# Turned rows and exponentials by way of HBM for nearly all sequences, in an attention and mixture-of-experts kernel

## The chip, the core and the metric

The kernel runs on one core of a Trainium2 chip. The metric is the device time of one execution in microseconds; each kernel is executed several times and the median counts. All times below are in microseconds unless marked ns.

## The reference

One layer with a norm ahead of each half: causal attention with one head, then a mixture of experts with a shared expert. There are 8 sequences of 512 tokens, 256 features each, all in float32.

```
x = x + attention(layernorm(x), Wq, Wk, Wv)      # softmax(q k' / 16, causal) v
h = layernorm(x)
shared = (silu(h Wg') * (h Wu')) Wd'              # inner size 512
probs  = sigmoid(h Wr' + bias)                    # 8 experts, the best two are taken
routed = sum over the two: weight * ((silu(h G_e) * (h U_e)) D_e)
x = x + shared + routed
```

## The kernel before

**Stages.** After an opening in which Wq and Wk are folded into one matrix, a Python loop (L630) goes through the 8 sequences `b`. For each it does the attention row block by row block (`attend`, L458; 4 blocks of 128 tokens), normalizes the result into `hn`, turns it into `hT` (features on the partitions), prepares the next sequence (its scores, its values `v`), finds the two experts of each token (`route`, L486) and the places of its rows in a table by expert (`places_of`, L540), and sends each row twice to HBM by indirect DMAs of GpSimd (`dispatch`, L557), into `rows_h`. When all sequences are done, `plan_tiles` (L189) works out which expert takes which 256 or 128 rows, and the routed experts run over them (L900, L923); `fetch` (L841) brings their rows and `fetch_w` (L831) their weights. Last come the shared expert of the sequences 4 to 6 and the sums.

**Units.** The shared expert of half a sequence is one unit (`shared_beside`, L564): 32 matmuls L578, the tanh form of silu on ScalarE (L589) and VectorE (L593, L596), 16 matmuls L605 and two copies L609 (each matmul instruction stands in the trace as two). The sequences 0, 1, 2, 3 and 7 give two units each to the list `waiting`. Each sequence takes one unit from the list and runs it between its own pieces. Sequence 0 has no older one, so it takes the first half of its own. Before the change, sequence 6 takes none; sequence 7 takes one, and three are left for L817, after the last `dispatch` and beside the plan.

**Two ways to turn.** A tile is turned either on TensorE (`turned`, L331, transposes L340 and a copy on ScalarE L341) or by way of HBM: it is stored (`stored_rows`, L370), loaded in 32-row blocks by four DMAs (`loaded_blocks`, L373) and finished by a transpose of 32x32 squares on VectorE (`turn_squares`, L382). The exponentials of the softmax likewise: on TensorE within `attend` (L463, L465), or with `ex_d`, `loaded_squares` (L418) and `turn_exponentials` (L430, L434). Three sets say which sequences go by HBM:

- `VIA` = 1 to 5 and 7: their `hn` goes by HBM, at least its first half.
- `WHOLE` = 1 to 5: both halves of `hn` do.
- `SENT` = 1 to 6: their exponentials do. Then all four scores of a sequence are done one stage earlier, behind the attention of the sequence before (L716), and `attend` finds its exponentials turned.

So before the change sequences 0 and 6 turn all of `hn` on TensorE, sequence 7 turns the second half there, and sequences 0 and 7 turn their exponentials there, with their scores between (L669).

**Order.** A scheduler orders the instructions of each engine when the kernel is built; `tc.issue_after(x)` sets what an instruction must stand behind. Each engine issues in that order. SP issues nearly all plain DMAs of the loop, GpSimd the indirect ones and the power of the norm (L179), ScalarE the expert weights. PSUM tiles come from three small pools: `ps_o` with 2 buffers holds the attention's output `av` (L472), freed by L476 on VectorE, and also the routing's tiles, the places `pp` (L544, L545) and the units' `po`; `ps_m` has 4 and `ps_t` 2. `marks["turned"]` holds back L476 behind the routing's last step on VectorE (`run`, L535).

**Start of the experts.** `fetch(0)` reads rows from `rows_h`, and so waits for all indirect stores and the rows of blanks (L199). The first turn L873 stands behind the last unit's L596 on VectorE; the next expert weights (L838) stand behind the last unit's L609 on ScalarE, and behind these the load of the table for silu.

## Time and profile before

| | us |
|---|---|
| median of 11 runs | 678.93 (678.24 to 680.88) |
| the profiled execution | 681.02 |
| its span, first to last instruction | 679.2 |
| TensorE matmul busy | 666.2 |
| VectorE busy | 302.4 |
| GpSimd busy | 157.6 |
| ScalarE busy | 150.9 |

The span is divided into 40 equal slices of 17 in the page; each digit is the busy share of a slice in tenths, PEclk the clock that TensorE was granted, DMA the mean share of the 16 DMA engines.

```profile
PE   6999999999999999999999999999999999999997
DVE  4668778787787753222122122121221112223765
PEclk9999999999999999999999999999999999999999
DMA  6643877768663266975653553554534557724875
```

The loop over the sequences fills about 13 slices (to 231), the units left over two more, the routed experts from 263 on the next 20 or so, and the late shared expert and the sums the rest. TensorE is busy throughout; VectorE is so only in the loop and at the end. A profile line gives start, busy time, engine, line and operation, then the tile written and those read, the shape, and how many; in brackets stands the idle time before it and what ended that.

### The profile page before, as it was taken

The numbers are of one execution on the slowest core, as the hardware profiler recorded it, in microseconds if no ns is written. First come the engines' busy times: TensorE is split into PE (matmuls) and PEld (weight loads), VectorE is DVE, ScalarE is ACT, GpSimd is POOL, SyncE is SP. The second block draws the span as 40 slices with busy tenths as digits, with TensorE's granted clock in tenths as the row PEclk, the third lists the DMA queues.
The fourth block names the chain that finished last, engine by engine and source line by source line (L and its number), as shares of the span: only waits on it lengthen the run. The fifth ranks groups of instructions, "written<-read, shape, count | busy, mean of one in ns | idle before, by whom it ended". The sixth has DMA issues, their size and how long they took to land.

```text
span 679.2 us, 10379 instructions
## 1 busy us (share of the span) xinstructions
PE 666.2 (98%) x3178; PEld 543.9 (80%) x3178; DVE 302.4 (45%) x1002; ACT 150.9 (22%) x359; POOL 157.6 (23%) x210
## 2 busy tenths in 40 slices
PE   6999999999999999999999999999999999999997
PEld 5677877777776888888888888888888899994556
DVE  4668778787787753222122122121221112223765
ACT  2432321322213222111211111111112111111110
POOL 3102451523516530021211211211121122121000
PEclk9999999999999999999999999999999999999999
DMA  6643877768663266975653553554534557724875
GB/s 232 180 119 110 237 201 179 207 171 221 203 155 110 91 190 166 305 203 164 187 179 119 164 174 113 177 162 127 179 132 130 158 171 225 249 97 144 239 233 176
DMA packets 152809, 118.48 MB, mean 174 GB/s; under 512 B 109648, under 2 KB 131280, under 8 KB 152752
## 3 DMA queue, kind: packets, MB, share of 16 engines
q1 hardware_dynamic: 133552, 57.00, 32.4%
q10 hardware_dynamic: 12912, 43.53, 18.5%
q0 software_dynamic: 6288, 17.24, 7.0%
q8 instruction: 28, 0.46, 0.3%
q14 instruction: 29, 0.24, 0.1%
HBM read 82.79 MB, written 34.95 MB: 173 GB/s over the span
## 4 chain that ended last, share of the span: by engine, by line
PE 78%; DVE 8%; DMA 5%; SPq 3%; POOL 2%; issue 2%; ACTq 1%; ACT 1%; DVEq 0%; POOLq 0%
PE po L923 17%; PE pg L900 17%; PE pu L900 17%; PE pg L578 6%; PE pg L1011 3%; PE po L605 3%; PE po L1070 3%; PE pu L1011 3%; PE pm L395 2%; PE sc L442 2%; PE av L472 2%; PE pm L407 2%; SPq L377 2%; SPq L424 2%; DMA squares<-exd 1%
## 5 line engine op out<-in xcount | busy, mean ns | idle before, releaser
L886 DVE TENSOR_TENSOR hidp<-pu,sgt 128x512 f32<-128x512 f32 x56 | 38.6, 691 | 210.2 <-PE pu L900 203.7
L929 POOL DMA_INDIRECT rows_y<-y,to x56 | 53.7, 959 | 266.0 <-ACT y L928 141.4
L900 PE MATMUL pg<-hTt,w 128*128 128x256 f32 x448 | 105.9, 379 | 0.8 <-ACT sgt L885 0.8
L900 PE MATMUL pu<-hTt,w 128*128 128x256 f32 x448 | 105.8, 379 | 0.0
L923 PE MATMUL po<-w_down,hidp 128*128 x448 | 101.3, 379 | 0.0
L900 PEld LDWEIGHTS pg<-hTt,w 128*128 128x128 f32 x448 | 85.0, 190 | 12.7 <-ACT sgt L885 1.2
L900 PEld LDWEIGHTS pu<-hTt,w 128*128 128x128 f32 x448 | 85.1, 190 | 11.6
L923 PEld LDWEIGHTS po<-w_down,hidp 128*128 128x128 f32 x448 | 85.0, 190 | 11.5
L578 PE MATMUL pg<-hT,w_sh 128*128 128x256 f32 x320 | 74.0, 383 | 0.2 <-ACT hT L341 0.2
L559 POOL DMA_INDIRECT rows_h<-hn,at x64 | 63.3, 988 | 22.7 <-issue 17.6
L885 ACT ACTIVATE sgt<-pg 128x512 f32<-128x512 f32 x67 | 40.0, 598 | 126.7 <-PE pg L900 119.8
L578 PEld LDWEIGHTS pg<-hT,w_sh 128*128 128x128 f32 x320 | 59.5, 190 | 9.5 <-ACT sg L589 0.8
L928 ACT COPY y<-po 128x256 f32<-128x256 f32 x67 | 24.8, 372 | 151.5 <-PE po L923 143.2
L179 POOL TENSOR_TENSOR rstd<-var,minus_half 128x1 f32<-128x1 f32 (+1 forms) x43 | 26.9, 634 | 129.4 <-DVE var L178 73.7
L605 PE MATMUL po<-w_sh,hid 128*128 128x256 f32 x160 | 37.3, 383 | 0.2
L442 PE MATMUL sc<-xT,qT 128*128 128x128 f32 (+3 forms) x128 | 37.4, 434 | 0.0
L605 PEld LDWEIGHTS po<-w_sh,hid 128*128 128x128 f32 x160 | 29.4, 190 | 6.1 <-DVE hid L596 2.1
L395 PE MATMUL pm<-xT,w_qk 128*128 128x512 f32 x64 | 29.9, 592 | 0.0
L886 DVE TENSOR_TENSOR khid<-pu,sgt 128x512 f32<-128x512 f32 x11 | 7.6, 691 | 48.9 <-PE pu L900 48.9
L407 PE MATMUL pm<-wv_sb,xT 128*128 128x256 f32 x128 | 29.0, 380 | 0.2 <-ACT xT L341 0.2
L407 PEld LDWEIGHTS pm<-wv_sb,xT 128*128 128x128 f32 x128 | 24.2, 190 | 6.1 <-issue 2.6
L172 DVE BATCH_NORM_STATS2 bnst<-total 128x6 f32<-128x256 f32 x64 | 25.2, 411 | 8.5 <-DMA total<-in_x_dram 8.5
(156 smaller groups left out, 760.7 us busy)
## 6 DMA issues: line engine op xcount, KB each, us to landing
w<-in_gate_w_dram ACTq DMA_DIRECT2D x41, 512.0 KB
w<-in_up_w_dram ACTq DMA_DIRECT2D x41, 512.0 KB
yl<-rows_y SPq DMA_DIRECT2D x32, 256.0 KB
h<-rows_h SPq DMA_DIRECT2D x112, 64.0 KB
w_down<-in_down_w_dram SPq DMA_DIRECT2D x8, 512.0 KB
out_dram<-total SPq DMA_DIRECT2D x32, 128.0 KB
total<-in_x_dram SPq DMA_DIRECT2D x7, 512.0 KB
xnd<-xn SPq DMA_DIRECT2D x6, 512.0 KB
```

The source lines that it names most:

```text
L395: nc.tensor.matmul(pm, lhsT=w_qk[:, k, ts(m, P)], rhs=xT[:, k, :], start=(k == 0), stop=(k == ND - 1),)
L407: nc.tensor.matmul(pm, lhsT=xT[:, k, ts(c, P)], rhs=wv_sb[:, k, :], start=(k == 0), stop=(k == ND - 1),)
L442: nc.tensor.matmul(sc[:, :n], lhsT=qT[:, k, ts(i, P)], rhs=xT[:, k, :n], start=(k == 0), stop=(k == ND - 1),)
L559: lands(nc.gpsimd.indirect_dma_start(out=rows_h[:, :], out_offset=bass.IndirectOffsetOnAxis(ap=at[:, r, c : c + 1], axis=0), in_=hn[:, c, ...
L578: mm = nc.tensor.matmul(pg[:, w, :], lhsT=w_sh[:, ds(w * gu + k * I + m * P, P)], rhs=hT[:, k, at], start=(k == 0), stop=(k == ND - 1),)
L605: nc.tensor.matmul(po, lhsT=hid[:, m, ts(j, P)], rhs=w_sh[:, ds(2 * gu + m * D, D)], start=(m == 0), stop=(m == NI - 1),)
L885: nc.scalar.activation(sg, pg, AF.Silu)
L886: return nc.vector.tensor_tensor(out=hid, in0=pu, in1=sg, op=ALU.mult).ins
L900: nc.tensor.matmul(dst[:, m, :], lhsT=w[:, i, k, ts(m0 + m, P)], rhs=hT[:, ts(k, n * P)], start=(k == 0), stop=(k == ND - 1),)
L923: nc.tensor.matmul(po, lhsT=hid[:, m, ts(j, P)], rhs=w_down[:, ds(w + m * D, D)], start=(m == 0), stop=(m == NI - 1),)
L929: nc.gpsimd.indirect_dma_start(out=rows_y[:, :], out_offset=bass.IndirectOffsetOnAxis(ap=to[:, j : j + 1], axis=0), in_=y, in_offset=None,)
L1011: nc.tensor.matmul(dst, lhsT=w_sh[:, ds(off + k * I + m * P, P)], rhs=hT[:, k, :], start=(k == 0), stop=(k == ND - 1),)
```

## The change

The sets change: `hn` goes by HBM whole for the sequences 0 to 6, and not at all for 7; exponentials go by HBM for 1 to 7. Sequence 6 now also takes a unit from the list, so two are left at the end in place of three. With that the special cases for sequence 6 go (its routing was run through at once, L776), and sequence 7, which now finds its scores done and has no sequence behind it, gets some of its own: no projection in its attention (`ahead_T is not None`), places of sequence 6 at row block 2, and the unit beside sequence 7 held back behind its first four matmuls (one half of `pg`, step `(0, 1)`) and no longer behind its eighth. All eight indirect stores of sequence 6 now stand at the last row block of sequence 7 (L700), in place of two at block 2 and six at block 3.

```
-    VIA = [b for b in range(1, B) if b != B - 2]
-    WHOLE = range(1, B - 2)
-    SENT = range(1, B - 1)
+    VIA = range(B - 1)
+    WHOLE = range(B - 1)
+    SENT = range(1, B)
...
             if i:
-                with tc.issue_after(summed.ins) if i != NT // 2 or xb is not total[B - 1] else nullcontext():
+                with tc.issue_after(summed.ins):
                     normalize(hn[:, i - 1, :D], xb, i - 1, mv, rstd)
...
-                with tc.issue_after(marks["turned"]) if r and b < B - 2 else nullcontext():
+                with tc.issue_after(marks["turned"]) if r and b < B - 1 else nullcontext():
                     nc.vector.tensor_reduce(out=top, in_=prob, axis=AX.X, op=ALU.max)
...
-                    elif (m, w) == (NI // 2 - 1, 1) and halfway is not None:
+                    elif (m, w) == (0, 1) and halfway is not None:
                         held = halfway
...
                 if b in SENT:
                     sc = exs[i]
-                    if i % 2 == 0:
+                    if i % 2 == 0 and ahead_T is not None:
...
-                if i == (1 if b in SENT else 2) and placed is not None:
+                if i == (1 if b in SENT and ahead_T is not None else 2) and placed is not None:
                     placed()
...
-                        with tc.issue_after(marks["blocks"]) if b else nullcontext():
+                        with tc.issue_after(marks["blocks"]) if b in WHOLE else nullcontext():
                             stored = nc.sync.dma_start(out=ex_d[b + 1][0], in_=ex[0]).ins
...
                 next(routing)
-                if b < B - 2:
+                if b < B - 1:
                     yield
                 mask = next(routing)
...
                 choice = chosen()
                 next(choice)
-                if b + 2 == B:
-                    for _ in choice:
-                        pass
...
             if b + 1 < B:
 
-                if b + 2 < B:
-                    def behind():
+                def behind():
...
-                    added = shared_beside(
-                        *waiting.pop(0), midway=midway, behind=behind, early=choice,
+                added = shared_beside(
+                    *waiting.pop(0), midway=midway, behind=behind, early=choice,
...
```

The last two pieces move `behind`, `midway` and the call of `shared_beside` out of a condition that left out sequence 6; their bodies stay.

More of the change, by code (lines that the diff above doesn't have):

```diff
@@ L786, with midway @@
             if b + 1 < B:
-                if b + 2 < B:
-                    def behind():
-                        nonlocal exT
-                        with tc.issue_after(marks["hid"]), tc.issue_after(marks["first"]):
-                            exT = turn_exponentials(squares)
-                        next(choice, None)
-                        marks["squares"], marks["turned"] = marks["turned"], marks["run"]
-                    def midway():
-                        if b + 3 < B:
-                            with tc.issue_after(marks["squares"]):
-                                rows, _ = first_norm(*coming)
-                            with tc.issue_after(marks["sent"]):
-                                blocks[b + 3], _ = sent_to_blocks(xn_d[b + 3], rows)
-                    added = shared_beside(
-                        *waiting.pop(0), midway=midway, behind=behind, early=choice,
-                        rows_from=1 if b in WHOLE else NI,
-                        steps=((NI // 2, 1), (NI - 1, 1)) if b in WHOLE else ((0, 1), (1, 1)),
-                    )
+                def behind():
+                    nonlocal exT
+                    with tc.issue_after(marks["hid"]), tc.issue_after(marks["first"]):
+                        exT = turn_exponentials(squares)
+                    next(choice, None)
+                    marks["squares"], marks["turned"] = marks["turned"], marks["run"]
+                def midway():
+                    if b + 3 < B:
+                        with tc.issue_after(marks["squares"]):
+                            rows, _ = first_norm(*coming)
+                        with tc.issue_after(marks["sent"]):
+                            blocks[b + 3], _ = sent_to_blocks(xn_d[b + 3], rows)
+                added = shared_beside(
+                    *waiting.pop(0), midway=midway, behind=behind, early=choice,
+                    rows_from=1 if b in WHOLE else NI,
+                    steps=((NI // 2, 1), (NI - 1, 1)) if b in WHOLE else ((0, 1), (1, 1)),
+                )
                 xT = ahead_T
```

## The prediction, made before the changed kernel was run

> **What bounds the kernel now.** I read the page first, then TensorE's waits, then the order of time on TensorE (PE), VectorE (DVE), ScalarE (ACT), GpSimd (POOL) and SyncE (SP) where the change acts. A "stage" below runs from the first scores of one sequence to those of the next.

> ```profile
> span 679.2 us, 10379 instructions
> PE 666.2 (98%) x3178; PEld 543.9 (80%) x3178; DVE 302.4 (45%) x1002; ACT 150.9 (22%) x359; POOL 157.6 (23%) x210
> ```

> PE is busy 98% of the span, and what it waits for after the opening loads is short:

> ```profile
> PE pt L463 <- ACT ex L451: 1.0, 2, 0.6
> PE pg L900 <- ACT sgt L885: 0.8, 1, 0.8
> PE pp L544 <- DVE total L476: 0.4, 1, 0.4
> ```

> So PE's order sets the end: an instruction taken from it is worth its start-to-start time, and a new wait on it costs its length. PE in order of time, around sequence 0 and around the last one (columns: start, busy time, engine and line):

> ```profile
> 34.39 4.48 PE L442 MATMUL sc<-xT,qT 128*128 128x128 f32 x16
> 38.70 3.62 PE L407 MATMUL pm<-wv_sb,xT 128*128 128x256 f32 x16
> 42.16 1.11 PE L340 MATMUL pt<-ident,hn 128*128 128x128 f32 x8
> 43.47 2.05 PE L578 MATMUL pg<-hT,w_sh 128*128 128x256 f32 x8 [0.20 <-ACT hT L341]
> ...
> 63.07 4.48 PE L442 MATMUL sc<-xT,qT 128*128 128x128 f32 x16
> ...
> 90.28 4.48 PE L442 MATMUL sc<-xT,qT 128*128 128x128 f32 x16
> ```

> ```profile
> 202.05 0.61 PE L442 MATMUL sc<-xT,qT 128*128 128x128 f32 x4
> ...
> 227.87 0.27 PE L500 MATMUL pl<-ident,logits 128*128 128x128 f32 x1
> ...
> 263.40 1.89 PE L900 MATMUL pg<-hTt,w 128*128 128x256 f32 x8
> ...
> 271.25 1.99 PE L900 MATMUL pg<-hTt,w 128*128 128x256 f32 x8 [0.77 <-ACT sgt L885]
> ```

> The reader is to see three marks of the last stage: A = 202.05 (its scores begin), pl = 227.87 (its routing logits), and 263.40 (the routed experts begin, after three whole units of shared expert). After 271.25 PE runs without a recorded wait to 613.58, so what is gained or lost before the experts stays to the end.

> **Step 1, sequence 0's rows by HBM.** Stage 0 lasts 63.07 - 34.39 = 28.68, stage 1 lasts 90.28 - 63.07 = 27.21; the 1.47 between them are the 8 transposes L340 and the wait for their copies (43.47 - 42.16 = 1.31) and small change. They go. But stage 0's unit takes sequence 0's own rows (nothing older waits in the list), so its first L578 stands right behind the values, 7.77 after the stage's start, and now needs the first half of the rows back from HBM. In stage 1 that half is turned here:

> ```profile
> 72.19 0.71 DVE L384 STREAM_TRANSPOSE hT<-blocks 128x512 f32<-128x512 f32 x1 [2.04 <-DMA blocks<-hnd]
> ```

> which is 9.12 after the stage's start. The last row is normalized (L325) 2.53 into stage 0 (36.92) and 2.93 into stage 1 (66.00), so the trip starts 0.4 earlier: turn at 8.72, L578 at 9.45, a wait of 1.7. That is the upper bound. The lower one: the loads' issues end 0.4 earlier than stage 1's 68.84, so 5.37 in; the fetch at 251.17 below, of the same size, has moved its data 1.7 after its last issue; 7.1 plus 0.71 gives L578 at 7.9, a wait of 0.1. In stage 1 the DMA engines are busy all the time from 70 to 74 (share 1.00, 330 GB/s) the indirect stores of the sequence before among it; in stage 0 from 38 to 42 it is 0.30, and there is no sequence before. So I take 0.7, nearer the lower. **Step 1: -1.47 + 0.7 = -0.8**, from -1.4 to +0.2. The ten new DMA issues of this stage (two stores of 0.38, eight loads of 0.48, 4.6 in all) stand on SP ahead of sequence 1's exponentials; their reloads (L424, 41.63 to 47.15 before) come some 3 later, and their first reader was at 52.83: covered.

> **Step 2, from A to pl.** Before: 227.87 - 202.05 = 25.82. After, in the built order: all four scores, the values, a whole unit beside, then row by row the attention of sequence 7, in which the only other work is the last unit's. Start to start from stage 5 (174.84 to 193.85): scores, values, 12 L578, routing, 4 L578 and 8 L605 take 19.01. Then 4 L578 of the next unit (1.73) to 20.74, and L472 of rows 0 and 1 (1.29) to 22.03. Row 2 needs the PSUM buffer of row 0, which L476 frees on DVE, and L476 stands behind the routing. Stage 5's DVE rows:

> ```profile
> 193.38 0.98 DVE L434 STREAM_TRANSPOSE exTs<-squares 128x768 f32<-128x768 f32 x1
> 194.71 0.71 DVE L434 STREAM_TRANSPOSE exTs<-squares 128x512 f32<-128x512 f32 x1 [0.35 <-DMA squares<-exd]
> ...
> 197.33 0.48 DVE L476 SCALAR_TENSOR_TENSOR total<-av,inv,total 128x256 f32<-128x256 f32 x1
> ...
> 200.88 0.48 DVE L476 SCALAR_TENSOR_TENSOR total<-av,inv,total 128x256 f32<-128x256 f32 x1
> ```

> In stages 1 to 5 a projection (L395, 1.72) stands between rows 1 and 2 and hides most of this; in the last stage there is none. Worse, in the built order the next unit's L593 and L596 stand between the two L434. L593 waits for ACT's tanh: L578 done at 20.74, tanh 0.2 later and 0.38 long, so L593 at 21.35, L596 at 21.8, the second L434 at 22.15, and from there as in stage 5 (197.33 - 194.71 = 2.62) L476 of row 0 at 24.77 to 25.25. **PE waits 25.3 - 22.03 = 3.3.** Row 2 (1.29) and the places' two matmuls (0.37) run to 26.97. Row 3 needs row 2's buffer: in stage 5 L476 of row 2 comes 3.55 after that of row 0, behind the POOL's power; some 0.5 of that is the places' work, which now stands later, so 27.85 to 28.3. **PE waits 1.4.** Row 3 (1.73) to 30.08, 8 L578 (3.45) to 33.53, which hide the last row's norm (2.86 behind row 3's end before: 221.46 to 224.32), then 8 transposes where there were 4 (0.95 for 0.46), L578, routing, L578 as before (2.50): pl at 36.98. **Step 2: 36.98 - 25.82 = +11.16.** Of this 10.36 is the unit that now stands here (253.04 - 242.68); without the two waits it would be +6.5. Saved here: 8 L340 (1.30), 10 L463 (1.35), and waits of 1.0, 0.4 and 0.3. Unsure: the rows' second half may come 0.3 late, and the DVE order may cost 1 less or more: +10 to +12.2.

> The sequence 6 indirect stores, spread before, now go in one run behind row 3's power (8 x 1.27 from about 32.7 to 42.8); sequence 7's places are ready 7.7 after pl, at 44.7, so POOL is free by 1.9.

> [...]

> **Step 3, from pl to the experts.** Before it is 263.40 - 227.87 = 35.53, all of it PE work. The other chain to the same point is hidden by it:

> ```profile
> 245.13 0.96 POOL L559 DMA_INDIRECT rows_h<-hn,at  x1 [0.31 <-issue]
> 251.17 1.96 SPq L851 DMA_DIRECT2D h<-rows_h  x4
> 261.36 1.29 DVE L873 STREAM_TRANSPOSE hTt<-h 128x512 f32<-128x512 f32 x2
> ```

> The last indirect store goes out at 245.13, SP may fetch at 251.17, and the DMA rates of the window 250 to 262 (40 slices of 0.3) show that first fetch over at 254.8, with the 16th slice:

> ```profile
> GB/s 0 0 0 0 0 0 0 105 109 76 140 130 104 166 44 7 1 73 135 127 112 112 89 131 85 18 0 65 161 183 45 106 127 170 16 35 1 0 70 144
> ```

> Then the turn (0.71) waits only for its place in DVE's order. It could end at 256.0, 28.1 after pl. After the change PE has one unit less between: 35.53 - 10.36 = 25.17. So PE waits 2.9 for the first tokens, and **step 3 is 28.1 - 35.53 = -7.43.** Bounds: 25.17 (chain hidden anyway) and 30 (fetch disturbed by weights that now load beside it).

> **Step 4, the start of the experts.** ACT issues the next weights and loads its table only behind the last L609 (264.18 to 270.60), which made PE late at 271.25 by 0.94 (268.58 + 1.73 = 270.31). With PE waiting 2.9 before the experts, that ends in time: **-0.9**, but up to +1 if those loads queue behind the tokens'.

> **Sum:** -0.8 + 11.16 - 7.43 - 0.9 = **+2.0**. The profiled execution (681.02, of which the span is 679.24) stands 2.1 over the median of the runs, 678.93; the difference goes onto the median: **681.0**, with a range of its own of 679 to 683.5. The 1.8 around the span stays.

> [...] The page before shows full clock in all slices, with no later wait over 0.8. [...]

> **Rivals.**
> (a) The token chain is hidden after all: step 3 becomes -10.36 and step 4 zero, sum 0.0, 678.9. For it: 1.8 of the 28.1 is SP's wait after the stores that might shrink. Against: every link is serial and was measured. 0.18.
> (b) The last attention does not wait: if the buffers came free in time, step 2 is +6.5 and the sum -2.7, 676.2. It is faster than the bound from the point where the two waits sum to under 1.3 in place of 4.7. For it: in stages 1 to 5 PE waited for L476 once, 0.45. Against: they have the projection there. 0.14.
> (c) All round trips at their upper bounds (step 1 +0.2, step 3 30 after pl): +4.9, 683.9. For it: stages 2 to 4 last 27.9 to 28.5, not 27.2, with the DMA engines crowded. 0.13.
> The forecast keeps 0.55.

> **Numbers.** About 0.2% (1.4 us) is what a measurement tells from no change. Slower: 0.13 of (c) and 0.50 of the forecast's 0.55, 0.63. Within: (a) and the rest, 0.23. Faster: 0.14. The range reaches from below (a) to (c), leaving (b) out: 677.8 to 684.

> **What would show it.** Step 1: the L578 behind the values 0.1 to 1.7 late, on DMA or DVE. Step 2: PE waiting for L476 before rows 2 and 3 of the last sequence, 3.3 and 1.4. Step 3: a wait of PE at the first L900 for L873, with SP's fetch as the releaser. Step 4: no wait at the third L900 group. It is wrong if DVE reaches L476 of row 0 by 22.1 after A, or if the first fetch is over 25 after pl.

## The result, and the profile after

| | before | after |
|---|---|---|
| median of the runs on the same chip, us | 679.62 (46 runs) | 688.14 (12 runs) |
| ratio, 95% interval | | 1.0129 [1.0116, 1.0142] |
| profiled execution, us (span) | 681.02 (679.2) | 685.92 (684.1) |

The change makes the kernel 8.5 us slower; the forecast was 2.0 (681.0, range 677.8 to 684.0). The profiled execution after is faster than all twelve runs (686.39 and more), the one before lies 1.4 above its median, so the two spans differ by 4.9 only. In some of the later sets of experiments the kernel before takes 684 to 687 and not 679; every ratio below is against its runs in the same set, and profiles are compared within 679 sets or within 684 to 687 sets.

The page of the changed kernel: span, the engines' busy times, and the granted clock in 40 slices.

```profile
span 684.1 us, 10366 instructions
PE 666.0 (97%) x3156; PEld 543.1 (79%) x3156; DVE 305.1 (45%) x1003; ACT 148.8 (22%) x356; POOL 156.9 (23%) x210
PEclk9999999999999998999999999999999999999999
```

PE's busy time has not changed: there are 22 transposes fewer, but two groups (below) ran at half speed. Its idle time has grown from 13.0 to 18.1, and one slice, the 16th, is below full clock. The waits of the changed kernel on PE (line, releaser, us in total, times, longest):

```profile
PE av L472 <- DVE total L476: 4.1, 2, 3.1
PE pg L896 <- DVE hTt L869: 2.9, 1, 2.9
PE po L919 <- issue: 1.5, 1, 1.5
```

The first two were forecast (3.3 and 1.4; 2.9). The third was not. PE in order of time (start, busy, line; the wait before it in brackets):

```profile
219.90 1.46 PE L472 MATMUL av<-v,exTs 128*128 128x256 f32 x6
224.46 1.56 PE L472 MATMUL av<-v,exTs 128*128 128x256 f32 x6 [3.10 <-DVE total L476]
...
236.13 0.27 PE L500 MATMUL pl<-ident,logits 128*128 128x128 f32 x1
...
264.66 3.78 PE L896 MATMUL pg<-hTt,w 128*128 128x256 f32 x8 [2.86 <-DVE hTt L869]
268.24 3.09 PE L896 MATMUL pu<-hTt,w 128*128 128x256 f32 x8
271.16 1.89 PE L896 MATMUL pg<-hTt,w 128*128 128x256 f32 x8
272.89 1.89 PE L896 MATMUL pu<-hTt,w 128*128 128x256 f32 x8
...
615.99 1.97 PE L919 MATMUL po<-w_down,khid 128*128 x8 [1.46 <-issue]
```

The first two groups of the experts take 3.58 and 2.92 from start to start, the next 1.73: half speed, at a granted clock of 0.50 from 263.82 to 270.65. The fifth group (the second tile) starts at 274.61. Cut at these marks, the profiles add up as follows. The right-hand pair is both kernels profiled again in one set, where before has a median of 684.8:

| stretch on PE | before | after | difference | second pair | forecast |
|---|---|---|---|---|---|
| start to stage 0 | 34.39 | 32.67 | -1.72 | +1.24 | 0 |
| stages 0 to 5 | 167.66 | 166.48 | -1.18 | -2.66 | -0.8 |
| last scores to logits (A to pl) | 25.82 | 36.98 | +11.16 | +11.41 | +11.16 |
| logits to the experts | 35.53 | 28.53 | -7.00 | -5.26 | -7.43 |
| first to fifth group | 7.85 | 9.95 | +2.10 | +1.94 | -0.9 |
| fifth group to the late sequences (L1007) | 342.33 | 343.93 | +1.60 | +2.54 | 0 |

The first row is chance: openings of 32.3 to 34.8 stand in the profiles of both kernels and of all variants. Without it the first pair shows +6.7 over these stretches. Two terms of the forecast are wrong, and both lie behind the first tokens. At the first of them, VectorE's turns and, in windows of 4 us, the busy times (PE, its weight loads, VectorE, ScalarE, GpSimd, with the number of instructions), PEclk, DMA share and GB/s of the changed kernel:

```profile
263.90 0.71 DVE L869 STREAM_TRANSPOSE hTt<-h 128x512 f32<-128x512 f32 x1 [4.22 <-DMA h<-rows_h]
...
270.75 0.71 DVE L869 STREAM_TRANSPOSE hTt<-h 128x512 f32<-128x512 f32 x1 [5.57 <-DMA h<-rows_h]
```

```profile
260.00:264.00 4.00, 1.80 (x9) 1.24 (x7) 0.10 (x1) 0.77 (x2) 0.00 (x0) 0.98 0.56 90
264.00:268.00 4.00, 3.34 (x8) 2.71 (x9) 1.18 (x2) 0.00 (x0) 0.00 (x0) 0.50 1.00 326
268.00:272.00 4.00, 4.00 (x14) 3.31 (x13) 0.71 (x1) 0.67 (x1) 0.00 (x0) 0.67 0.88 250
```

The second tile's tokens come 6.85 after the first's, at a DMA share of 1.00. Before the change, the row at 261.36 shown in the prediction was two turns (x2, 1.29): both tiles were ready before the experts began. ScalarE, which issues the next tiles' weights, loads its table and then makes the first gate, before:

```profile
264.18 0.34 ACTq L838 DMA_DIRECT2D w<-in_gate_w_dram  x1
...
269.30 1.28 ACT L885 ACT_TABLE_LOAD   x1 [5.32 <-DMA w<-in_up_w_dram]
...
270.60 1.09 ACT L885 ACTIVATE sgt<-pg 128x512 f32<-128x512 f32 x2
```

and after, with the fifth group on PE:

```profile
262.42 0.34 ACTq L834 DMA_DIRECT2D w<-in_gate_w_dram  x1
...
263.79 0.34 ACTq L834 DMA_DIRECT2D w<-in_gate_w_dram  x1
268.66 0.34 ACTq L834 DMA_DIRECT2D w<-in_up_w_dram  x1
...
271.33 1.28 ACT L881 ACT_TABLE_LOAD   x1 [9.11 <-DMA tail<-rows_h]
272.63 1.09 ACT L881 ACTIVATE sgt<-pg 128x512 f32<-128x512 f32 x2
...
274.61 1.89 PE L896 MATMUL pg<-hTt,w 128*128 128x256 f32 x8
```

From the first of these issues to the gate it takes 6.4 before and 10.2 after.

### The profile page after: what moved, and what is told of

It is laid out like the page before. It is cut to its first block, busy times and chain, and to the rows that moved or that the text cites. A ratio compares the mean times of both kernels' runs of the same rounds, so it can differ in the third digit from the quotient of the medians.

```text
span 684.1 us, 10366 instructions
## 1 busy us (share of the span) xinstructions
PE 666.0 (97%) x3156; PEld 543.1 (79%) x3156; DVE 305.1 (45%) x1003; ACT 148.8 (22%) x356; POOL 156.9 (23%) x210
## 4 chain that ended last, share of the span: by engine, by line
PE 79%; DVE 10%; DMA 4%; SPq 3%; issue 2%; POOL 1%; ACT 0%; ACTq 0%; DVEq 0%; POOLq 0%
PE pg L896 17%; PE pu L896 17%; PE po L919 17%; PE pg L578 6%; PE pg L1007 3%; PE po L1066 3%; PE pu L1007 3%; PE sc L442 2%; PE po L605 2%; PE av L472 2%; PE pm L407 2%; PE pm L395 2%; SPq L377 2%; DMA blocks<-hnd 2%; DVE bnst L172 1%
## 5 line engine op out<-in xcount | busy, mean ns | idle before, releaser
L896 PE MATMUL pg<-hTt,w 128*128 128x256 f32 x448 | 107.7, 384 | 2.9 <-DVE hTt L869 2.9
L896 PE MATMUL pu<-hTt,w 128*128 128x256 f32 x448 | 107.0, 382 | 0.0
L919 PE MATMUL po<-w_down,hidp 128*128 x448 | 101.3, 379 | 0.0
L896 PEld LDWEIGHTS pg<-hTt,w 128*128 128x128 f32 x448 | 86.1, 193 | 15.2 <-DVE hTt L869 3.3
L896 PEld LDWEIGHTS pu<-hTt,w 128*128 128x128 f32 x448 | 86.1, 192 | 12.0
L919 PEld LDWEIGHTS po<-w_down,hidp 128*128 128x128 f32 x448 | 85.0, 190 | 11.5
L578 PE MATMUL pg<-hT,w_sh 128*128 128x256 f32 x320 | 73.9, 383 | 0.2 <-issue 0.2
L881 ACT ACTIVATE sgt<-pg 128x512 f32<-128x512 f32 x67 | 39.9, 597 | 127.4 <-PE pg L896 123.1
L578 PEld LDWEIGHTS pg<-hT,w_sh 128*128 128x128 f32 x320 | 59.8, 190 | 9.7 <-ACT sg L589 0.8
L559 POOL DMA_INDIRECT rows_h<-hn,at x64 | 62.6, 978 | 20.5 <-issue 17.5
L605 PE MATMUL po<-w_sh,hid 128*128 128x256 f32 x160 | 37.8, 384 | 0.3
L472 PE MATMUL av<-v,exTs 128*128 128x256 f32 x140 | 33.4, 384 | 4.1 <-DVE total L476 4.1
L442 PE MATMUL sc<-xT,qT 128*128 128x128 f32 (+3 forms) x128 | 36.7, 434 | 0.0
L605 PEld LDWEIGHTS po<-w_sh,hid 128*128 128x128 f32 x160 | 29.1, 190 | 7.2 <-DVE hid L596 2.8
L472 PEld LDWEIGHTS av<-v,exTs 128*128 128x128 f32 x140 | 26.0, 190 | 10.4 <-DVE total L476 4.6
L589 ACT ACTIVATE sg<-pg 128x256 f32<-128x256 f32 x40 | 15.3, 384 | 68.7 <-PE pg L578 56.5
L395 PE MATMUL pm<-xT,w_qk 128*128 128x512 f32 x64 | 30.1, 592 | 0.0
## 6 DMA issues: line engine op xcount, KB each, us to landing
yl<-rows_y SPq DMA_DIRECT2D x32, 256.0 KB, 3.3
hnd<-hn SPq DMA_DIRECT2D x14, 256.0 KB, 2.2
```

The lines of the kernel that those rows point to most:

```text
L395: nc.tensor.matmul(pm, lhsT=w_qk[:, k, ts(m, P)], rhs=xT[:, k, :], start=(k == 0), stop=(k == ND - 1),)
L442: nc.tensor.matmul(sc[:, :n], lhsT=qT[:, k, ts(i, P)], rhs=xT[:, k, :n], start=(k == 0), stop=(k == ND - 1),)
L472: mixed = nc.tensor.matmul(av, lhsT=exT[:, ts(j, P)], rhs=v[:, j, :], start=(j == 0), stop=(j == i))
L559: lands(nc.gpsimd.indirect_dma_start(out=rows_h[:, :], out_offset=bass.IndirectOffsetOnAxis(ap=at[:, r, c : c + 1], axis=0), in_=hn[:, c, ...
L578: mm = nc.tensor.matmul(pg[:, w, :], lhsT=w_sh[:, ds(w * gu + k * I + m * P, P)], rhs=hT[:, k, at], start=(k == 0), stop=(k == ND - 1),)
L605: nc.tensor.matmul(po, lhsT=hid[:, m, ts(j, P)], rhs=w_sh[:, ds(2 * gu + m * D, D)], start=(m == 0), stop=(m == NI - 1),)
```

## The experiments

The ratio is to the kernel before in the same set, with its interval.

**Is it the clock?** Matmuls that nobody reads fill the waits (before the experts, before rows 2 and 3, both).

```
+        def spin(n):
+            pt = ps_t.tile([P, S], F32, tag="t", name="spin")
+            for _ in range(n):
+                mm = nc.tensor.matmul(pt[:, : S // 2], lhsT=w_sh[:, ts(0, P)], rhs=w_sh[:, ds(0, S // 2)], start=True, stop=True)
+            return mm.ins
...
+        with tc.issue_after(marks["po"]):
+            spin(12)          # fill_start; 6 in fill_exact
...
+                if b == B - 1 and i >= 2:
+                    with tc.issue_after(mixed):
+                        mixed = spin({2: 13, 3: 4}[i])   # fill_rows; 7 and 2 in fill_exact
```

> The changed kernel with 12 more 128x256 matmuls on TensorE (about 12 x 0.216 = 2.6 us) between the last shared unit and the experts, where it waited 2.86 for its first tokens; their result is read by nobody. Theory 1 (the wait halves the granted clock, and the two first expert groups of 3.58 and 2.92 us are slow for that): the wait before L896 shrinks to under 0.5, the four first groups take 1.73 each, the mean clock rises by 0.005 or more, and the median falls from 688.1 by 3 to 3.5, to about 684.8. Theory 2 (the first groups are slow because weights or tokens come in late, or because of the DMA traffic beside them): the groups stay slow, 688. If the added matmuls outlast the tokens, up to 0.3 is added in both.

> The changed kernel with 13 more matmuls before row 2 and 4 before row 3 of the last sequence's attention (2.8 and 0.9 us), where TensorE waited 3.10 and 1.02 for L476; their result is read by nobody. Theory 1: in the profiled run these waits left the clock whole, but runs of the changed kernel differ in mean clock (0.995, 0.992, 0.990 for 684, 687 and 689 us of span), so in some runs a second 3.4 us window at half clock falls here; with the gap filled no run is below 0.995 and the median falls by 1 to 3, to 685 to 687. Theory 2 (what more the other runs take lies elsewhere): 688 with the same spread of clocks.

> Both sets of added matmuls at once. Theory 1: every run at clock 1.000, the waits' own length still lost, so 688.1 less 3 to 3.5 less 1 to 3: 681.5 to 684; the forecast's 681.0 held the waits at full clock, so near 681 would say that the clock is all that it missed. Theory 2: 688.

Measured, in a set where before takes 687.4: 1.0062 [1.0040, 1.0085], 1.0094 [1.0063, 1.0124], 1.0094 [1.0075, 1.0114]. Each matmul took 0.43 and not 0.216: the trace shows it as two records, so a line of x8 is four instructions (and a unit, with its 32 and 16 records, is 16 and 8 instructions). The "two passes" in an expectation below are these two records. So the fillings lasted 5.3 and 5.8, twice the waits, and the ratios mix two things; taken as ratios to 679.6 the forecasts were 1.008, 1.008 to 1.011 and 1.003 to 1.006, and only the third is clearly missed. In fill_start the four first groups did take 1.73 each. The experiment was repeated with half as many, beside both kernels:

> The kernel before itself, profiled on the chip of this set, since one set ran on a chip where it takes 687.4 in place of 679.6. All theories: ratio 1.000. If this chip is the slower one, its profile tells where the 8 us go: more than 2 us of them in idle time named issue or remote on TensorE and ScalarE (as in the last set's records), or in the opening loads.

> The changed kernel itself. [...] Rival (each wait of about 3 us always costs the same): one clock in all runs.

> As the version with both sets of added matmuls, but with half as many: 7 before row 2, 2 before row 3 and 6 before the experts (one such matmul takes 0.43 us, two passes; the sets before were sized by one pass and lasted twice the waits). 3.0, 0.9 and 2.6 us, as long as the waits. [...] Rival (waits, not the clock): no change from the changed kernel, 1.010 to 1.014.

Measured: before_again 0.9995 [0.9976, 1.0013], after_again 1.0111 [1.0083, 1.0138], fill_exact 1.0128 [1.0101, 1.0155]. The changed kernel's four runs had mean clocks of 0.993, 0.993, 0.997 and 1.000, and took 694.4, 692.8, 693.9 and 692.4: the full clock bought almost nothing. In fill_exact the waits at rows 2 and 3 and at the first group are gone and the four first groups are at full speed; yet the fifth starts 9.75 after the first. PE and ScalarE there:

```profile
273.95 0.34 ACTq L849 DMA_DIRECT2D w<-in_gate_w_dram  x1
277.74 0.34 ACTq L849 DMA_DIRECT2D w<-in_up_w_dram  x1
278.11 1.28 ACT L896 ACT_TABLE_LOAD   x1 [9.82 <-DMA w<-in_up_w_dram]
...
280.05 2.73 PE L911 MATMUL pg<-hTt,w 128*128 128x256 f32 x8 [2.69 <-ACT sgt L896]
```

ScalarE stands in its weight issues until 278.08; only then come its table load and the gate that PE's fifth group waits for. The clock theory as the whole cause falls: what PE gains earlier, it waits for here. The before_again expectation of over 2 us of idle time named issue or remote found 1.0 on PE, but 49.4 and 8.0 on ScalarE (4.8 and none in the 679 profile); PE waits 1.7 for one of these stops. Against the 679 profile its stages 0 to 5 are 2.9 longer, A to pl 1.9 and pl to the experts 1.9; what makes those sets slower is open.

**Is it the waits before rows 2 and 3?**

```
-                with nullcontext() if early is None or ...
+                with tc.issue_after(marks["turned"]) if halfway is not None and m == 0 else nullcontext() if early is None or ...
```

> The changed kernel with one edit of VectorE's order: in the last sequence the unit's first L593 (and L596) is put behind the turn of the second half of the exponentials and the routing, so that L476 of row 0 no longer stands behind them. Theory 1 (the 3.10 before row 2 is this order): the wait before row 2 falls from 3.10 to 0.3 to 1.0, that before row 3 stays at 0.8 to 1.5, the routing logits and all behind them come 2.0 to 2.8 earlier; the wait for the first tokens stays at about 2.9, since its chain begins at the logits, and the clock there falls as before. Median 685 to 686. Rival (row 2 waits for something else, such as the exponentials' reload): no change, 688.

Measured 1.0019 [1.0004, 1.0035], in the set of 687.4. The wait before row 2 is 0.53 (3.10), before row 3 1.21, A to pl 35.44 (39.11 in after_again). The mechanism of step 2 is shown. The gain is larger than the wait: with it goes the half clock in the rows behind (L472 of rows 2 and 3 take 1.56 and 1.99, in after_again 2.93 and 3.08), and the fifth group comes 7.01 behind the first (8.84). The changed kernel itself was not run in this set.

**What stands in the chain from the logits to the first tokens?** In the second profile of the changed kernel ScalarE's L609 came late, and VectorE's order put the addition L811 ahead of the mask:

```profile
248.09 0.66 ACT L609 ACTIVATE sh<-po 128x256 f32<-128x256 f32 x2 [5.30 <-remote]
248.78 0.69 DVE L811 TENSOR_TENSOR total<-total,sh 128x512 f32<-128x512 f32 x1 [2.14 <-ACT sh L609]
249.39 0.18 DVE L530 TENSOR_TENSOR mask<-hot,hot 128x32 f32<-128x32 f32 x1
249.72 0.38 PE L544 MATMUL pp<-mask,before 128*128 128x32 f32 x2 [2.78 <-DVE mask L530]
```

```
+        with tc.issue_after(marks["run"]):
             added()                             # mask_first
...
-            if t + AHEAD <= MEAN:
+            if 0 < t <= MEAN - AHEAD:           # late_w3: the fourth tile's loads
...
+            if t == 0:
+                with tc.issue_after(product):
+                    items.append(fetch(AHEAD)[1])
...
-                added = shared_beside(
+                if b == B - 2:                  # no_unit6
+                    next(choice)
+                    next(choice)
+                    behind()
+                added = None if b == B - 2 else shared_beside(
```

> The changed kernel with one edit of VectorE's order: the addition of the last sequence's unit to its total (L811), which waits for ScalarE's L609, goes behind the routing's mask (L530) and not ahead of it. In the changed kernel's second profile L609 came at 248.09, 5.3 after the instruction before it on ScalarE, L811 at 248.78 and the mask at 249.39, and TensorE waited 2.78 for it. Theory 3 (the token chain is long because the mask stands behind an addition that nobody needs yet): from the routing logits to the experts 32.2 becomes 29 to 30, as in the changed kernel's first profile (28.5), TensorE's wait for L530 under 0.5, and the ratio falls by 0.002 to 0.004, to 1.007 to 1.010. Rival (that wait is covered by the wait for the first tokens that follows it anyway): from the logits to the experts unchanged, ratio 1.010 to 1.014.

> The changed kernel with the fourth tile's loads (weights on ScalarE's queue, tokens on SyncE's) issued behind the first tile's gate product and no longer ahead of it. In the profiles ScalarE's two issues of those weights wait until 279.95 (277.74, 270.96 in others), and only behind them stand the table load and the first L881, for which the third group of matmuls waits 1.7 to 2.7. Theory 4 (the start of the experts is set by ScalarE's issues, not by the clock): no wait for L881 over 0.5, from the first to the fifth group 6.9 to 7.3 in place of 8.8 to 10 (up to 10 if a half-clock window falls there), ratio down by 0.002 to 0.003. Rival (the clock sets it): no change.

> The changed kernel without a unit beside sequence 6: both transposes by HBM stay, and the unit goes back to where it stood before, between the last attention and the experts. Forecast by step 3: the experts start 35.5 to 37.5 after the logits with no wait for tokens (-10.36 + 2.9 + 10.36), the waits before rows 2 and 3 shrink since no L593 of a unit stands between the two L434; but sequence 6's reload and turn have no unit to stand beside, and TensorE waits some 10 there, for L384 and L434. Sum: ratio 1.008 to 1.018. If the unit is not what covers those round trips, TensorE waits under 4 there and the ratio is under 1.005.

> Three edits of order on top of the changed kernel: VectorE's L593 of the last unit behind the routing of sequence 6 (2.0 to 2.8 less before row 2), the mask ahead of L811 (up to 2.8), the fourth tile's loads behind the first product (1.5 to 2.5). If they add up: 5.5 to 8 less than the changed kernel, a ratio of 1.000 to 1.004. If each only moves the wait on to the next one in the chain to the first tokens: above 1.006.

Measured, before at 679.2: mask_first 1.0130 [1.0107, 1.0154]; late_w3 1.0118 [1.0097, 1.0139]; no_unit6 1.0131 [1.0114, 1.0148]; mended 1.0040 [1.0025, 1.0056].

mask_first missed: in this set L609 was not late (L544 waits 0.3 in all four profiles), so its theory had nothing to remove; from the logits to the experts 27.0, and the fifth group gave it back (9.06, of it 1.9 for ScalarE). late_w3 took the wait for L881 away, as expected, but half clock lay on its first group (3.52 for 1.73): first to fifth 8.70, no gain. In no_unit6 the unit went back, the experts start 35.9 behind the logits without a wait, as expected, and the waits came where the unit had stood (6.7 in place of some 10):

```profile
PE av L472 <- DVE exTs L434: 4.0, 1, 4.0
...
PE lT L492 <- DVE hT L384: 2.7, 2, 1.6
```

So the unit covers a round trip at either place, and there is one unit for two. mended, with all three edits, is 6 us below mask_first and late_w3 of its set. Since those two alone bought nothing, the reordered L593 carries most of it, by itself or together with them: A to pl is 34.54, the clock is whole in the profile, and PE waits 1.6 for the first tokens and as long again at the fifth group, where the profile names no releaser but the second turn ends 0.1 before:

```profile
269.13 0.71 DVE L870 STREAM_TRANSPOSE hTt<-h 128x512 f32<-128x512 f32 x1 [7.40 <-DMA w<-in_up_w_dram]
...
269.94 1.97 PE L897 MATMUL pg<-hTt,w 128*128 128x256 f32 x8 [1.55 <-issue]
```

**Tokens against weights, and the wait at the end.**

```
         weights = fetch_w(0)
+        sooner = [fetch_w(t) for t in range(1, AHEAD)]        # early_w, mended3
...
-            items += [fetch(t)[1] for t in range(1, AHEAD)]
+            items += [fetch(t, w)[1] for t, w in zip(range(1, AHEAD), sooner)]
...
+            warm = ps_o.tile([P, P], F32, tag="o", name="warm")   # mended3_warm, after_warm, mended_warm
+            for _ in range(12):
+                nc.tensor.matmul(warm, lhsT=ident, rhs=ident, start=True, stop=True)
```

> The changed kernel with the weights of the second and third tiles loaded beside the last shared unit and no longer behind it, ahead of the first tokens. Theory 5 (the start of the experts is set by the DMA engines: in the profiles the tokens of the second tile and 2 MB of weights are all moved between 264 and 271 at a DMA share of 1.00, and the second turn L869 comes at 270.75, 7 us after the first; before the change both turns stood ahead of the experts): the second turn comes within 4 us of the first, no wait at the fifth group of matmuls, first to fifth group 6.9 to 7.3 (plus up to 1.7 for a half-clock window), ratio down by 0.003 to 0.005 from 1.012. Against it, up to 2 us: the weights may slow the last indirect stores or the first tokens, so that the wait before the first group grows from 2.9. Rival (the clock alone): first to fifth group stays at 8.5 to 10.

> All four edits of order on top of the changed kernel: L593 behind the routing, the mask ahead of L811, weights of the second and third tiles sooner, the fourth tile's loads later. The version with three of them stood at 1.004, with first to fifth group 8.73 and a wait of 1.6 for the first tokens. If the second tile's tokens are what was left there: first to fifth group 6.9 to 7.3, ratio 1.000 to 1.003. If the weights then hold up the first tokens: 1.003 to 1.006.

> As the version with four edits, with 12 matmuls of the identity with itself at TensorE's very start, where it waits 4.0 for the first weights; nobody reads them. Two things are looked at. First, the wait of 1.5 to 2.2 named issue before the last L919: it stands in all profiles of the changed kernel whose TensorE program has at most 2163 instructions, and in none with 12 or more added; if it belongs to where the program's pieces lie in memory it is gone here (-1.5 to -2), if it belongs to the change's work it stays. Second, the clock at the start: full clock begins at 7.8 to 11.8 in the profiles; with TensorE at work from 1.5 it should begin one or two windows earlier, -0.5 to -2. Together a ratio 0.002 to 0.006 below that of the version without them; neither: the same or +0.5 us.

> The changed kernel with the 12 matmuls of the identity at TensorE's start and nothing else. In the version with four edits they took away the wait named issue before the last L919 (1.9, from the fifth group of the experts to the late sequences 344.4 to 342.2) and moved the median by only -0.7 with few runs. If that wait is a full term of the loss: 1.5 to 2 less than the changed kernel, ratio 1.009 to 1.0105, from the fifth group on 342.3. If the time is lost elsewhere in other runs: 1.011 to 1.013.

> The best version so far (three edits of order: L593 behind the routing, the mask ahead of L811, the fourth tile's loads later; 1.004) with the 12 matmuls at the start. If the wait at the last L919 goes here too: 1.001 to 1.002, what is left being the wait for the first tokens (1.6) and the second tile's tokens (1.6). It does not beat the kernel before unless the start gains as well (0 in the version with four edits).

Measured: early_w 1.0162 [1.0126, 1.0198], mended3 1.0097 [1.0075, 1.0120], mended3_warm 1.0092 [1.0072, 1.0113], before at 678.5; after_warm 1.0058 [1.0036, 1.0079], mended_warm 0.9952 [0.9935, 0.9970], before at 687.3. Weights that load sooner make it worse: the wait for the first tokens grows from 2.9 to 4.9 (early_w), from 1.6 to 4.5 (mended3), and the second turn still comes 7.2 (early_w, 276.73 after 269.49) and 6.9 (mended3) after the first. That tokens and weights crowd each other is in line with both directions; that the fifth group would come in time was wrong, and mended3 lies above both of its forecasts.

The 12 matmuls at the start remove the wait at the last L919 in all three kernels that have them (fifth group to late sequences 342.2, 342.2, 341.5). The four filled kernels, with 12 to 29 matmuls more, do not have it either. The ten profiles of the changed kernel and its other variants all have it, 1.46 to 2.23, and each time it ends within 0.05 of the start of a 16 KB transfer of the trace's instruction queue (after: 615.97, PE resumes at 615.99). That the change's work does not make this wait is shown, since after_warm does all of it and more; that the number of instructions ahead decides fits all 20 profiles; what PE waits for there is not shown. The 12 matmuls also bring full clock earlier (from 5.4 to 7.0, where it was 7.8 to 11.8), but no earlier first stage.

after_warm and mended_warm lie below their forecasts (1.009 and more; 1.001 and more), and why is open. mended_warm beats the kernel before in its set, by 0.5%. It was not run in a set where before takes 679, and the kernel before was not run with the 12 matmuls, so how much of this the changed order earns is open.

**The two parts by themselves.** seq0 is the kernel before with `VIA = [b for b in range(B) if b != B - 2]`, `WHOLE = range(B - 2)` and the change's `if b in WHOLE` at L719; last is the changed kernel with both from 1 on.

> Step 1 alone: the kernel before with sequence 0's rows by HBM, the last two sequences and the shared units left as they were. Forecast by step 1: -0.8 (-1.4 to +0.2), ratio 0.9988 (0.998 to 1.0003), stage 0 at 27.2 to 28.9 in place of 28.68, clock 1.000 in all runs. Rival (part of the 8.5 comes from here): ratio over 1.002.

> The changed kernel without its sequence 0 part: sequence 0's second half is turned by TensorE as before, sequences 6 and 7 go by HBM, the unit stands beside sequence 6. The sequence 0 part alone measured 1.0002 (0.9985 to 1.002). If the two parts only add: 1.010 to 1.015. If sequence 0's part holds up the later sequences (its ten more DMA issues): below 1.010.

Measured: seq0 1.0002 [0.9985, 1.0020], with a stage 0 of 27.66; last 1.0147 [1.0117, 1.0177]. The loss is in the part on sequences 6 and 7.

## Why the prediction was right in direction and wrong in size

**Step 1 held.** Stage 0 fell from 28.68 to 27.61, -1.07 (forecast -0.8); PE's wait behind the values was 0.16, not 0.7. By itself the part is worth nothing that can be measured (seq0, 1.0002): against before_again of the same set its stage 0 is 1.0 shorter, and the stretch from the fifth group on 1.0 longer, 0.8 of it a wait named issue before the last L923.

**Step 2 held to the last digit in the profiled run, +11.16,** with its two waits (3.10 and 1.02 for 3.3 and 1.4) and their cause. But the run was lucky. In the four other profiles of 679 sets with this wait of 3.1 (late_w3, last, mask_first, early_w, alike in the last stage up to pl) A to pl is 37.5, 37.7, 39.3 and 39.4, 38.5 in the mean: half clock follows the wait (L472 of row 2 takes 2.58, 2.35, 2.20 and 1.91 there, in the profiled run 1.56), and those 0.5 to 2.5 us are not in the sum.

**Step 3 held for the first tile,** -7.00 for -7.43, wait 2.86 for 2.9; late_w3, mask_first and last take 27.0 to 29.1 from pl to the experts, for 28.1.

**Step 4 is the step that failed.** It said that the weights' issues and the table load end in time, since PE starts later (-0.9, at worst +1), and so left ScalarE's 6.4 from its first issue to the gate as they were. Measured +2.10 and +1.94: that chain takes 10.2, 9.3, 9.1 and 10.0 in after, after_again, mask_first and last. The path was followed to the first tile's tokens only. Before, three units of shared work covered the tokens of two tiles; with one unit less, the second tile's tokens are fetched while 2 MB of weights load, and ScalarE stands in the issues (none from 264.13 to 268.66, at a DMA share of 1.00). That the missing unit is what does it is shown by no_unit6, which has it ahead of the experts again and keeps the rest of the change: both tiles are turned before the experts, ScalarE's chain takes 4.9, and the fifth group comes 6.91 behind the first without a wait. How tokens and weights hold each other up is not shown. A head start of the tokens goes with it: in dve_order and after_warm the second tile's tokens begin to go out 2.0 and 1.8 ahead of those weights (in the four above between 0.4 ahead and 0.6 behind), the chain takes 5.0 and 5.5, and the fifth group comes 7.01 behind the first. From pl to the fifth group the forecast was 28.1 + 6.9 = 35.0; the four profiles of the changed kernel or of it with one edit behind pl or in sequence 0 (after, late_w3, mask_first, last) show 38.5, 37.8, 36.1 and 37.0. In the first of them the half clock hides the wait for ScalarE's gate: it ends at about 273.2, so at full clock, as an estimate, the fifth group would have come at 273.3 and not at 274.6.

**A term that was not in the sum:** the wait before the last L919, +1.6 and +2.5. "After 271.25 PE runs without a recorded wait" held for the kernel before; the changed one has 22 records of PE fewer ahead of that place, and the wait goes when 12 matmuls are added.

Together, as an estimate: the 6.7 of the profiled pair without the opening, and some 1.5 for the clock behind row 2 that other runs pay (38.5 less 36.98), are 8.2 of the 8.5.

**The rivals.** Neither (a) nor (b) came about. (c), the upper bounds, was nearest in size with 683.9, and its bound of 30 from pl to the experts was exceeded in the slower sets (32.2 in the second profile), there with the mask behind L811.

## What to carry to other kernels

When a cover is taken away, follow the chain past the first thing that it hid to the second: here the wait for the first tile's tokens came as forecast (2.86), and the second tile's, fetched beside the weights, drew ScalarE's first gate from 6.4 to 10.2 behind its first issue. A wait of PE was not worth its length here: half clock behind the 3.10 before row 2 added 0.5 to 2.5 in four profiles and nothing in the first, and in fill_exact and mask_first a later wait (2.69 and 1.88) took back what had been gained ahead of it. A forecast has to price both. A change that saves PE's transposes but needs cover twice is worth what the order around it makes of it: with one instruction moved on VectorE 1.0019 was left, where the changed kernel has 1.0111 and 1.0129 in other sets.

## What the runs showed of the hardware

Over all 20 profiles, windows of 3.413 us, in step with the clock record of each, by the share of them in which PE was idle (worked out from the matmul records and the granted clock; the opening and the last 6 us left out):

```
idle share of a window    windows    followed by half clock
0.42 to 0.55              19         0
0.57 to 0.59               4         3   (0.58 once without)
0.66 to 1.00              21         21
```

Of the 22 stretches at half clock 14 are one window long, seven two and one three. The same gap of 3.10 before row 2 fell 0.44 and 0.47 into two windows in the first profile of the changed kernel (no effect) and 0.59 and 0.32 in the second (two windows, 6.8 us at half clock). Runs of one program differ by microseconds: in those of the changed kernel in the 679 set the span goes with the mean clock (684.1 to 687.6 at 0.995, 688.9 at 0.990), in those of after_again it does not (692.7, 691.0, 692.1 and 690.6 at 0.993, 0.993, 0.997 and 1.000).

ScalarE's stop of 5.3 to 5.4 before L609, released by nothing that the trace names, stands at the same place in all eight profiles of the changed kernel and its variants from the sets where before takes 684 to 687, and in none from the 679 sets. The kernel before has such stops elsewhere in such a set (before_again: 5.3 before L589, 2.7 before L465), seq0 has none. What they are stays open.
